# A four-layer graph network on one core: some transposes of the first and the last graphs by TensorE instead of through DRAM, and other turns at the end

## The chip, the cores and the metric

The kernel runs on one core of one Trainium2 chip. The metric is the device time of one execution in microseconds, as the median of several runs. Beside the runs there is one profiled execution, from which all busy times, waits and starts are taken.

A core has five engines that run at the same time, each with its own queue of instructions in a fixed order: PE (TensorE, matrix products, with a separate part for loading the stationary operand, PEld), DVE (VectorE), ACT (ScalarE, which needs a table load when it goes from one group of functions to another), POOL (GpSimd) and SP (SyncE, which here issues all DMAs). An instruction waits for semaphores that others raise; what stands behind it in its engine's queue waits too.

## The reference, cut to what matters

64 independent graphs of 256 nodes with 256 features pass through four layers. Everything is in 32-bit floating point. After each layer stands a residual sum and a layer norm.

```python
# layer 0: 4 heads, sigmoid attention, weighted by adj, normalized by the row sums
X, q, k = heads(lrelu(x @ W_lin + b)), heads(lrelu(x @ W_q)), heads(lrelu(x @ W_k))
adj_h = adj[:, None] * sigmoid(einsum('bhxd,bhyd->bhxy', q, k) * hd ** -0.5)
dis = deg ** -0.5                       # deg = adj_h.sum(-1), 0 where deg is 0
x = LN(x + LN(merge(dis[..., None] * adj_h * dis[..., None, :] @ X)) * g + b)
# layer 1: 8 heads, softmax attention masked by adj > 0
e = softmax(where(adj > 0, q @ k.T / sqrt(32), NEG))
x = LN(x + merge(e @ v) @ Wo + bo)
# layer 2: sum over neighbours, then a two-step network with RMS norm
agg = eps * x + adj @ x
x = LN(x + silu(rmsnorm(agg @ W1 + b1) * w) @ W2 + b2)   # W1 256 x 1024, W2 1024 x 256
# layer 3: additive attention, one head
Wh = x @ W;  e = leaky_relu(Wh @ a1 [:, None] + Wh @ a2 [None, :], 0.2)
x = LN(x + gelu(LN(softmax(where(adj > 0, e, NEG)) @ Wh) * gamma + beta))
```

## The kernel before, in words

**One graph.** `graph` writes down all operations of one graph `b`; a 256 x 256 matrix lies in one tile of 128 partitions with two halves of 256 elements side by side. Where a product needs its operand the other way round, the matrix has to be transposed. There are two ways in the code. `transposed` (L266) lets PE do it, as four products of 128 x 128 with the identity matrix (L263) into a PSUM tile, and `copy` (L297) has ACT bring that to SBUF (L299). `far_transposed` (L271) does it without PE: DVE transposes blocks of 32 x 32 (L275), and DMAs put the blocks in their places by way of a buffer in DRAM. For layer 3 these are four writes (L281) and four reads (L285); with `in_order=False`, for layer 0, one write (L289) and four reads (L291), and the two DVE products at L482 take up the order that is left.

Layer 0 gives the attention result of L475 to the second form (L478). Layer 1 makes the scores of four heads at a time (L510), DVE adds the mask and finds the least value (L395), ACT takes the exponential (L400), and each pair of heads goes through a DVE transpose (L521), one DRAM write of 512 KB (L523) and four reads of 128 KB (L525) before the product with v (L536). The reciprocals of the row sums are transposed by PE (L543) and spread over partitions through DRAM (L546, L549), L553 multiplies, and L319 applies Wo. Layer 2 is L567 (neighbours), L579 (W1), L609 and L613 (norm and SiLU), L622 (W2). Layer 3 sends its input through the first form (L628) and goes on with L637 (W and the two attention vectors), the exponentials (L400 again), a transpose of e by PE and ACT, the product with v, GELU (L661), the residual (L662), the last layer norm (L364) and the store (L664).

**The order of work.** `graph` only lists operations, with an estimated cost, the values that each reads and writes, and for those that need an ACT table a turn. `Plan.order` (L94) then makes one list for all 64 graphs before anything is emitted: it keeps a clock for each engine and always takes the operation that can start earliest by its estimates, the one with the earlier due time where they are equal. A due time is the least due time or turn of what comes after. `emit` (L714) writes the instructions in the order of the planned starts, and so each engine's queue is fixed.

A turn is `4 * min(b + ROUND[layer], plan.graphs - 1 + TAIL[layer]) + func`, with func 0 for sigmoid (layer 0), 1 for exponentials (layers 1 and 3), 2 for SiLU (layer 2), 3 for GELU (layer 3). ROUND = 0, 2, 5, 7 makes one round hold layer 0 of graph b, layer 1 of graph b - 2, layer 2 of b - 5 and layer 3 of b - 7, so that ACT changes its table once for each function and round. TAIL bounds the round at the end, so that the last graphs share turns: with 5 for layer 3, graph 60 has its exponentials in round 67 and graphs 61, 62 and 63 in round 68. An operation with a turn may not be planned before all ACT operations of earlier turns have been.

Operations that wait for nothing, which are the loads, are held back in another way:

```python
if (op.due - AHEAD if op.first else op.turn or 0) > turns[turn]:
    continue
```

AHEAD = 14 lets a load in when its due time is at most 14 turns away, where four turns are a round. Tiles come from pools with a fixed number of slots (SLOTS: 42 of the kind "s", 8 PSUM tiles "p", 8 DRAM buffers "h"), and an operation can't be planned before it has its slots.

Of the kernel before, what the change touches and what calls it, by code (L numbers as in the profile page):

```python
# [11 lines left out]
OP = mybir.AluOpType  # L12

P = 128
# [5 lines left out]
PE_MM, PE_TR = 432, 109  # L20
# [5 lines left out]
DMA_KB, DMA_SEEN = 4, 1900  # L26

WORDS = {"s": 516, "d": 1024, "b": 2048, "c": 32, "p": 512, "h": 1024}
AHEAD = 14

ROUND = 0, 2, 5, 7
TAIL = 0, 2, 3, 5
SLOTS = {"s": 42, "d": 10, "b": 3, "c": 72, "p": 8, "h": 8}


# [39 lines left out]
class Plan:  # L75
# [9 lines left out]
    def op(self, engine, cost, fn, w=(), r=(), turn=None, mode="full", after=None, size=0):  # L85
        pair = lambda x: x if isinstance(x, tuple) else (x, None)
        w, r = [pair(x) for x in w], [pair(x) for x in r]
        op = Op(engine, cost, fn, w, r, self.graph, turn, mode, after, size)
        op.table = turn is not None and engine == "ACT"
        if op.table:  # L90
            self.turns[turn] = self.turns.get(turn, 0) + 1
        self.ops.append(op)
# [73 lines left out]
def two(v):  # L166

    return v.t.rearrange("p (n c) -> p n c", n=2)
# [69 lines left out]
def graph(plan, nc, c, t, out, b):  # L238

    op = plan.op  # L240
    pe, dve, act, pool = nc and nc.tensor, nc and nc.vector, nc and nc.scalar, nc and nc.gpsimd
# [7 lines left out]
    def turn(layer, func):  # L249
        return 4 * min(b + ROUND[layer], plan.graphs - 1 + TAIL[layer]) + func  # L250

# [6 lines left out]
    def transpose(dst, src, w, r):  # L258

        def fn():  # L260
            for j in range(2):
                for i in range(2):
                    pe.transpose(dst()[:, j, i * P:(i + 1) * P], src()[:, i, j * P:(j + 1) * P], c.ident)  # L263
        op("PE", 4 * PE_TR, fn, [w], [r], mode="transpose")

    def transposed(src):  # L266
        ps = Value("p", "ps", 2)
        transpose(lambda: two(ps), lambda: two(src), ps, src)
        return ps

    def far_transposed(src, name, in_order=True):  # L271


        eb, far, dst = Value("s", "eb"), Value("h", "far", 4), Value("s", name, 4)
        op("DVE", 635, lambda: dve.transpose(  # L275
            eb.t.rearrange("p (b g i) -> p g b i", b=4, i=32),
            src.t.rearrange("p (n k w) -> p k n w", n=2, k=2)), [eb], [src])
        if in_order:
            F = lambda a: far.t[:64].rearrange("(a z) (y w) -> a (z y) w", a=4, w=P)[a]
            for a in range(4):  # L280
                op("SP", 420, lambda a=a: nc.sync.dma_start(  # L281
                    F(a).rearrange("(b j) w -> j b w", b=4),
                    eb.t[32 * a:32 * a + 32].rearrange("j (b w) -> j b w", b=4)), [(far, a)], [eb], after=3000, size=64)
            for a in range(4):
                op("SP", 420, lambda a=a: nc.sync.dma_start(  # L285
                    dst.t.rearrange("q (g a i) -> a q g i", g=4, a=4)[a],
                    F(a).rearrange("q (g i) -> q g i", g=4)), [(dst, a)], [(far, a)], after=4500, size=200)
            return dst
        op("SP", 420, lambda: nc.sync.dma_start(far.t[:, :512], eb.t), [(far, i) for i in range(4)], [eb], after=3000, size=256)  # L289
        for q in range(4):  # L290
            op("SP", 420, lambda q=q: nc.sync.dma_start(  # L291
                dst.t[32 * q:32 * q + 32].rearrange("j (a g) -> j a g", a=4),
                far.t[:, :512].rearrange("(a j) (b g) -> b j a g", a=4, b=4)[q]), [(dst, q)],
                [(far, i) for i in range(4)], after=4200, size=64)
        return dst

    def copy(ps, name):  # L297
        dst = Value("s", name, 2)
        op("ACT", 466, lambda: act.copy(dst.t, ps.t), [dst], [ps])  # L299
        return dst  # L300
# [109 lines left out]
    xT, adjT, x, adj = load("x0T", "xT"), load("adjT", "adjT"), load("x", "x"), load("adj", "adj")  # L410
    qk = []
    for w, name in ((c.w0_q, "qT0"), (c.w0_k, "kT0")):
        ps = feature_major(w, xT)
        y = Value("s", name)
# [3 lines left out]
    ps = token_major(xT, lambda: c.w0_l.t, [c.w0_l])  # L418
    v = Value("s", "v0")
# [20 lines left out]
    ps = Value("p", "ps")  # L440
# [18 lines left out]
    dp, dis = Value("c", "dp"), Value("c", "dis")  # L459
# [5 lines left out]
    by_head = lambda ap: ap.rearrange("p (g d) -> p g d", d=HD0)  # L465
    dis_b = lambda: dis.t[:, :8, None].to_broadcast([P, NB * H0, HD0])
    op("DVE", 603, lambda: dve.tensor_tensor(by_head(v.t), by_head(v.t), dis_b(), OP.mult), [v], [v, dis])
    ps = Value("p", "ps", 2)
# [6 lines left out]
                    pe.matmul(two(ps)[i * HD0:(i + 1) * HD0, hp, :], two(v)[:, m, h * HD0:(h + 1) * HD0],  # L475
                              A(h)[:, m, :], start=(m == 0), stop=(m == NB - 1))
    op("PE", 4 * PE_MM, fn, [ps], [v, att], mode="columns")
    yb = far_transposed(ps, "yT", in_order=False)  # L478
    y = Value("s", "y", 2)
    for i in range(2):  # L480
        by = lambda ap, i=i: ap.rearrange("p g (i k w) -> p g i k w", i=2, k=2)[:, :, i]
        op("DVE", 345, lambda y=y, i=i, by=by: dve.tensor_tensor(  # L482
            by(y.t.rearrange("p (g d) -> p g d", g=4)), yb.t.rearrange("p (i k g w) -> p i g k w", i=2, k=2, g=4)[:, i],
            dis.t[:, :8].rearrange("p (g i) -> p i g", i=2)[:, i, :, None, None].to_broadcast([P, 4, 2, 32]), OP.mult),
            [y], [yb, dis])
    mv, m = stats(y)
    affine(y, mv, m, c.g0, lambda n, xb=xb: two(xb)[:, n, :], [xb])
    x = normed(y, "x1")
# [5 lines left out]
    ps = feature_major(c.w1_q, xT)  # L494
# [5 lines left out]
    v1 = copy(token_major(xT, lambda: c.w1_v.t, [c.w1_v]), "v1")  # L500
    av, r = Value("p", "av", 2), Value("c", "r")
    eTs = []
    for hq in range(H1 // 4):
        pss = [Value("p", "ps", 2) for _ in range(4)]

        def fn(hq=hq, pss=pss):
            for n in range(NB):
                for i in range(4):
                    s = slice(i * HD1, (i + 1) * HD1)
                    pe.matmul(two(pss[i])[:, n, :], two(qT1)[s, hq, n * P:(n + 1) * P], two(kT1)[s, hq, :],  # L510
                              start=True, stop=True)
        op("PE", 2 * PE_MM, fn, pss, [qT1, kT1], turn=turn(1, EXP), mode="rows")
        for pair in range(2):


            e, eb, far, eT = Value("d", "e", 4), Value("d", "eb"), Value("h", "far"), Value("d", "eT", 4)
            for i in range(2):
                softmax(pss[2 * pair + i], negmask, HD1 ** -0.5, e,
                        lambda n, i=i, e=e: e.t[:, 256 * (2 * i + n):256 * (2 * i + n + 1)],
                        lambda n, i=i: 2 * i + n, r, lambda n, h=4 * hq + 2 * pair + i: 2 * h + n, turn(1, EXP))  # L520
            op("DVE", 1155, lambda e=e, eb=eb: dve.transpose(eb.t.rearrange("p (b g i) -> p g b i", b=4, i=32),  # L521
                                                             e.t.rearrange("p (g b i) -> p g b i", b=4, i=32)), [eb], [e])
            op("SP", 420, lambda eb=eb, far=far: nc.sync.dma_start(far.t, eb.t), [far], [eb], after=3500, size=512)  # L523
            for q in range(4):
                op("SP", 420, lambda far=far, eT=eT, q=q: nc.sync.dma_start(  # L525
                    eT.t[32 * q:32 * q + 32].rearrange("j (a g) -> j a g", a=4),
                    far.t.rearrange("(a j) (b g) -> b j a g", a=4, b=4)[q]), [(eT, q)], [far], after=4000, size=128)
            eTs.append(eT)


    def fn():
        for hq in range(H1 // 4):
            for m in range(NB):
                for i in range(4):
                    h = 4 * hq + i
                    pe.matmul(two(av)[i * HD1:(i + 1) * HD1, hq, :], two(v1)[:, m, h * HD1:(h + 1) * HD1],  # L536
                              eTs[h // 2].t.rearrange("p (a h n k i) -> p h k n a i", a=4, h=2, n=2, k=2)[:, i % 2, m],
                              start=(m == 0), stop=(m == NB - 1))
    op("PE", 4 * PE_MM, fn, [av], [v1, *eTs], mode="columns")

    op("DVE", 180, lambda: dve.reciprocal(r.t[:, :16], r.t[:, :16]), [r], [r])
    ps = Value("p", "ps")
    op("PE", PE_TR, lambda ps=ps: pe.transpose(ps.t[:16, :P], r.t[:, :16], c.ident), [ps], [r], mode="transpose")  # L543
    rT, far, rb = Value("s", "rT"), Value("h", "far"), Value("s", "rb", H1)
# [7 lines left out]
    yT = Value("s", "yT")  # L552
    op("DVE", 575, lambda: dve.tensor_tensor(yT.t, av.t, rb.t, OP.mult), [yT], [av, rb])  # L553
    x = normed(plus(token_major(yT, lambda: c.w1_o.t, [c.w1_o]), xb), "x2")

    adj2 = load("adj2", "adjT")
    for n in range(NB):
        d = lambda n=n: two(adj2)[:, n, n * P:(n + 1) * P]
# [4 lines left out]
    ps = Value("p", "ps", 2)  # L563
# [10 lines left out]
    for j in range(0, HB, 2):  # L574
        ps = Value("p", "ps", 2)
# [17 lines left out]
    ps = Value("p", "ps")  # L593
# [21 lines left out]
    ps = Value("p", "ps", 2)  # L615
# [9 lines left out]
    x = normed(plus(ps, xb), "x3")  # L625


    xT3 = far_transposed(x, "xT3")  # L628
    v3 = Value("s", "v3", 2)
    V3 = lambda: v3.full.rearrange("p (n c) -> p n c", n=2)  # L630
    s1 = lambda n: V3()[:, n, D:D + 1]
    for n in range(NB):
        ps = Value("p", "ps")
# [14 lines left out]
    e = Value("s", "e3", 2)  # L648
# [7 lines left out]
    eT = copy(transposed(e), "eT")  # L656
    ps = token_major(eT, lambda: V3()[:, :, :D], [v3])
    y3 = Value("s", "y", 2)
    mv, m = stats(ps, r3)
# [91 lines left out]
```

## Time and profile before

| | |
|---|---|
| median of 3 runs | 2822.43 us (2820.94 to 2826.75) |
| profiled execution | 2825.22 us |
| its span, first to last instruction | 2823.4 us |
| PE busy | 2752.3 us |
| DVE busy | 2494.3 us |
| ACT busy | 2131.5 us |
| mean DMA rate | 170 GB/s |
| DRAM reads and writes | 290.60 MB and 185.07 MB |
| mean granted PE clock | 0.991 |

In the lines of the timeline below, the first two numbers are start and duration in us, counted from the first instruction; then come the engine, the line of the code, the operation, what it writes and reads, its shape and how many of them follow each other. In brackets stand the engine's idle time just before, and what ended it. L numbers are lines of the kernel before. Busy times of PE are those of a pipeline and overlap a little; the granted clock is the share of its full speed that PE was given.

### The profile page before, as it was taken

The numbers are of one execution on the slowest core, as the hardware profiler recorded it, in microseconds if no ns is written. First come the engines' busy times: TensorE is split into PE (matmuls) and PEld (weight loads), VectorE is DVE, ScalarE is ACT, GpSimd is POOL, SyncE is SP. The second block draws the span as 40 slices with busy tenths as digits, with TensorE's granted clock in tenths as the row PEclk, the third lists the DMA queues.
The fourth block names the chain that finished last, engine by engine and source line by source line (L and its number), as shares of the span: only waits on it lengthen the run. The fifth ranks groups of instructions, "written<-read, shape, count | busy, mean of one in ns | idle before, by whom it ended". The sixth has DMA issues, their size and how long they took to land.

```text
span 2823.4 us, 55149 instructions
## 1 busy us (share of the span) xinstructions
PE 2752.3 (97%) x17092; PEld 2189.6 (78%) x17092; DVE 2494.3 (88%) x7757; ACT 2131.5 (75%) x5054; POOL 585.8 (21%) x902
## 2 busy tenths in 40 slices
PE   8899999999999999999999999999999999999996
PEld 6667777887787878788878878778787778777784
DVE  5788898989899998998899989899989989899975
ACT  3767787778688777877777777878768877686774
POOL 1011211212222222212212212222212221212111
PEclk9999999999999999999999999999999999999998
DMA  4857476646466646665576556556556647475641
GB/s 142 252 151 196 152 202 180 187 134 192 127 193 199 197 135 200 192 179 148 155 192 180 172 163 183 171 167 187 174 149 183 198 141 201 125 194 153 181 123 41
DMA packets 558613, 479.40 MB, mean 170 GB/s; under 512 B 184304, under 2 KB 516976, under 8 KB 558320
## 3 DMA queue, kind: packets, MB, share of 16 engines
q1 hardware_dynamic: 558320, 475.87, 59.2%
q8 instruction: 137, 2.24, 0.4%
q14 instruction: 156, 1.28, 0.2%
HBM read 290.60 MB, written 185.07 MB: 168 GB/s over the span
## 4 chain that ended last, share of the span: by engine, by line
PE 87%; DVE 5%; ACT 3%; DMA 2%; SPq 1%; issue 1%; POOL 0%; DVEq 0%; POOLq 0%; ACTq 0%
PE ps L622 15%; PE ps L308 15%; PE ps L319 14%; PE ps L579 14%; PE ps L510 4%; PE ps L432 4%; PE ps L567 4%; PE ps L637 4%; PE ps L475 3%; PE av L536 3%; PE ps L263 2%; ACT e L400 1%; PE ps L449 1%; DVE e L395 1%; DVE st L333 1%
## 5 line engine op out<-in xcount | busy, mean ns | idle before, releaser
L400 ACT ACTIVATE e<-e,low 128x256 f32<-128x256 f32 x1152 | 575.7, 501 | 73.5 <-DVE low L395 69.8
L622 PE MATMUL ps<-w,hT 128*128 128x256 f32 x2048 | 480.6, 382 | 4.2 <-ACT hT L613 4.2
L579 PE MATMUL ps<-aggT,w 128*128 128x256 f32 x2048 | 470.8, 382 | 2.8 <-ACT aggT L299 1.4
L345 POOL TENSOR_SCALAR mv<-mv 128x2 f32<-128x2 f32 x384 | 123.0, 320 | 1624.8 <-DVE mv L335 1074.0
L579 PEld LDWEIGHTS ps<-aggT,w 128*128 128x128 f32 x2048 | 382.4, 190 | 69.2 <-issue 8.6
L622 PEld LDWEIGHTS ps<-w,hT 128*128 128x128 f32 x2048 | 381.3, 190 | 67.6 <-issue 10.5
L395 DVE CUSTOM_DVE_ANT_0 e<-ps,adj 128x256 f32<-128x256 f32 x1024 | 361.7, 420 | 33.5 <-PE ps L510 32.5
L521 DVE STREAM_TRANSPOSE eb<-e 128x1024 f32<-128x1024 f32 x256 | 310.5, 1225 | 4.7 <-ACT e L400 4.0
L346 POOL TENSOR_TENSOR mv<-mv,mhalf 128x2 f32<-128x2 f32 x384 | 307.7, 801 | 32.0
L584 ACT ACTIVATE hT<-ps,b 128x256 f32<-128x256 f32 x512 | 225.8, 473 | 97.0 <-PE ps L579 66.6
L360 ACT ACTIVATE x<-y,mv 128x256 f32<-128x256 f32 x384 | 216.2, 599 | 61.3 <-DVE mv L356 53.2
L333 DVE BATCH_NORM_STATS2 st<-y 128x6 f32<-128x256 f32 x640 | 242.3, 412 | 1.4
L400 ACT ACTIVATION_READ_ACCUMULATOR e<-e,low 128x1 f32 x1152 | 220.8, 192 | 0.0
L609 DVE SCALAR_TENSOR_TENSOR hT<-hT,r,pr 128x256 f32<-128x256 f32 x512 | 207.3, 474 | 7.0 <-PE pr L606 6.6
L590 DVE TENSOR_TENSOR sq<-sq 128x512 f32<-128x512 f32 x192 | 130.5, 680 | 48.1 <-ACT sq L587 47.0
L438 DVE TENSOR_TENSOR att<-att,adjT 128x512 f32<-128x512 f32 x256 | 165.7, 678 | 5.6 <-ACT att L436 5.5
L587 ACT ACTIVATE sq<-hT 128x512 f32<-128x512 f32 x256 | 163.1, 637 | 2.0 <-DMA far<-eb 0.6
L510 PE MATMUL ps<-kT,qT 32*128 32x256 f32 x2048 | 152.0, 404 | 1.0 <-ACT kT L299 1.0
L462 POOL TENSOR_TENSOR dp<-dp,mhalf 128x8 f32<-128x8 f32 x64 | 109.2, 1707 | 202.7 <-DVE dp L461 175.4
L436 ACT ACTIVATE att<-ps 128x512 f32<-128x512 f32 x256 | 132.3, 603 | 25.0 <-PE ps L622 18.6
L613 ACT ACTIVATE hT<-hT 128x1024 f32<-128x1024 f32 x128 | 129.8, 1051 | 19.5 <-DVE hT L609 17.0
L308 PE MATMUL ps<-x0T,w_q 128*128 128x256 f32 x512 | 132.1, 392 | 7.2 <-DMA x0T<-in_xT 7.2
(108 smaller groups left out, 5526.7 us busy)
## 6 DMA issues: line engine op xcount, KB each, us to landing
far<-eb SPq DMA_DIRECT2D x256, 512.0 KB, 3.5
eT<-far SPq DMA_DIRECT2D x1024, 128.0 KB, 3.9
adj<-in_adj SPq DMA_DIRECT2D x128, 256.0 KB, 4.7
x0T<-in_xT SPq DMA_DIRECT2D x64, 256.0 KB, 3.5
adjT<-in_adjT SPq DMA_DIRECT2D x64, 256.0 KB, 4.4
x<-in_x SPq DMA_DIRECT2D x64, 256.0 KB, 4.8
adj<-in_adjT SPq DMA_DIRECT2D x64, 256.0 KB, 5.3
far<-eb SPq DMA_DIRECT2D x64, 256.0 KB, 2.7
```

What stands on the lines that cost most here:

```text
L308: pe.matmul(two(ps)[:, o, :], w.t[:, k, o * P:(o + 1) * P], two(xT)[:, k, :], start=(k == 0), stop=(k == DB - 1))
L319: pe.matmul(two(ps)[:, n, :], two(xT)[:, k, n * P:(n + 1) * P], w()[:, k, :], start=(k == 0), stop=(k == DB - 1))
L333: op("DVE", 328, lambda n=n: dve.bn_stats(st.t[:, 6 * n:6 * n + 6], two(src)[:, n, :]), [(st, n)], [(src, n)])
L346: pool.tensor_tensor(m()[:, :, 2], m()[:, :, 2], c.mhalf[:, :NB], OP.pow)
L360: op("ACT", 492, lambda n=n: act.activation(two(dst)[:, n, :], two(src)[:, n, :], AF.Identity, bias=m()[:, n, 0:1], scale=m()[:, n, 2:3]), ...
L395: op("DVE", 345, lambda n=n: dve.tensor_tensor_reduce(out=E(n), in0=two(logits)[:, n, :], in1=two(negmask)[:, n, :], scale=-scale, scalar= ...
L400: op("ACT", 491, lambda n=n: act.activation(E(n), E(n), AF.Exp, bias=low.t[:, n:n + 1], scale=-1.0, accum_out=r.t[:, col(n):col(n) + 1]), ...
L510: pe.matmul(two(pss[i])[:, n, :], two(qT1)[s, hq, n * P:(n + 1) * P], two(kT1)[s, hq, :], start=True, stop=True)
L521: op("DVE", 1155, lambda e=e, eb=eb: dve.transpose(eb.t.rearrange("p (b g i) -> p g b i", b=4, i=32), e.t.rearrange("p (g b i) -> p g b i" ...
L579: pe.matmul(two(ps)[:, i, :], c.w2_1.t[:, k, (j + i) * P:(j + i + 1) * P], two(aggT)[:, k, :], start=(k == 0), stop=(k == DB - 1))
L584: op("ACT", 357, lambda ps=ps, i=i, j=j: act.activation(Hb(j + i)[:, 0], two(ps)[:, i, :], AF.Identity, bias=c.b2_1.t[:, j + i:j + i + 1]) ...
L622: pe.matmul(two(ps)[:, n, :], Hb(j)[:, 0, n * P:(n + 1) * P], c.w2_2.t[:, j, :], start=(j == 0), stop=(j == HB - 1))
```

## The change

It sets new numbers and puts the other kind of transpose in three places. `NEAR = 1, 1, 3` says for how many graphs: layer 0 and layer 1 of the first graph (b = 0), layer 3 of the last three (61, 62, 63). All other graphs keep their way through DRAM.

In layer 0 of graph 0, ACT copies the result to SBUF, PE transposes it, and one DVE product with `dis` reads it from PSUM. In layer 1 of graph 0, each head of a pair is transposed by four PE transposes into PSUM and copied by ACT; eT then has another order of elements, so each entry of `eTs` now carries a function that picks its part. In layer 3 of the last three graphs, PE and ACT replace the whole of `far_transposed`. TAIL's last number goes from 5 to 4, so that graphs 60 to 63 all have layer 3 in round 67. AHEAD goes from 14 to 12 turns.

```diff
-AHEAD = 14
+AHEAD = 12
+NEAR = 1, 1, 3
 
 ROUND = 0, 2, 5, 7
-TAIL = 0, 2, 3, 5
+TAIL = 0, 2, 3, 4
...
     op("PE", 4 * PE_MM, fn, [ps], [v, att], mode="columns")
-    yb = far_transposed(ps, "yT", in_order=False)
     y = Value("s", "y", 2)
-    for i in range(2):
...
+    if b < NEAR[0]:
+        ps = transposed(copy(ps, "yT"))
+        op("DVE", 602, lambda ps=ps, y=y: dve.tensor_tensor(by_head(y.t), by_head(ps.t), dis_b(), OP.mult), [y], [ps, dis])
+    else:
+        yb = far_transposed(ps, "yT", in_order=False)
...
+            if b < NEAR[1]:
+                eT = Value("d", "eT", 2)
+                for i in range(2):
+                    half = lambda v, i=i: v.t[:, 512 * i:512 * (i + 1)].rearrange("p (n c) -> p n c", n=2)
+                    ps = Value("p", "ps", 2)
+                    transpose(lambda ps=ps: two(ps), lambda e=e, half=half: half(e), ps, e)
+                    op("ACT", 466, lambda ps=ps, eT=eT, half=half: act.copy(half(eT), two(ps)), [(eT, i)], [ps])
+                eTs.append((eT, lambda i, m, eT=eT: eT.t.rearrange("p (h m c) -> p h m c", h=2, m=2)[:, i, m]))
+                continue
...
-            eTs.append(eT)
+            eTs.append((eT, lambda i, m, eT=eT: eT.t.rearrange("p (a h n k i) -> p h k n a i", a=4, h=2, n=2, k=2)[:, i, m]))
...
-                              eTs[h // 2].t.rearrange("p (a h n k i) -> p h k n a i", a=4, h=2, n=2, k=2)[:, i % 2, m],
+                              eTs[h // 2][1](i % 2, m),
...
-    xT3 = far_transposed(x, "xT3")
+    xT3 = copy(transposed(x), "xT3") if b >= plan.graphs - NEAR[2] else far_transposed(x, "xT3")
```

More of the change, by code (lines that the diff above doesn't have):

```diff
@@ L477, in graph @@
     op("PE", 4 * PE_MM, fn, [ps], [v, att], mode="columns")
-    yb = far_transposed(ps, "yT", in_order=False)
     y = Value("s", "y", 2)
-    for i in range(2):
[L481 to L485, printed above, removed]
+    if b < NEAR[0]:
[4 more added lines that the diff above has]
+        for i in range(2):
+            by = lambda ap, i=i: ap.rearrange("p g (i k w) -> p g i k w", i=2, k=2)[:, :, i]
+            op("DVE", 345, lambda y=y, i=i, by=by: dve.tensor_tensor(
+                by(y.t.rearrange("p (g d) -> p g d", g=4)), yb.t.rearrange("p (i k g w) -> p i g k w", i=2, k=2, g=4)[:, i],
+                dis.t[:, :8].rearrange("p (g i) -> p i g", i=2)[:, i, :, None, None].to_broadcast([P, 4, 2, 32]), OP.mult),
+                [y], [yb, dis])
     mv, m = stats(y)
@@ L513, in graph @@
         for pair in range(2):
-            e, eb, far, eT = Value("d", "e", 4), Value("d", "eb"), Value("h", "far"), Value("d", "eT", 4)
+            e = Value("d", "e", 4)
             for i in range(2):
@@ L520, in graph @@
                         lambda n, i=i: 2 * i + n, r, lambda n, h=4 * hq + 2 * pair + i: 2 * h + n, turn(1, EXP))
+            if b < NEAR[1]:
+                eT = Value("d", "eT", 2)
+                for i in range(2):
+                    half = lambda v, i=i: v.t[:, 512 * i:512 * (i + 1)].rearrange("p (n c) -> p n c", n=2)
[4 more added lines that the diff above has]
+                continue
+            eb, far, eT = Value("d", "eb"), Value("h", "far"), Value("d", "eT", 4)
             op("DVE", 1155, lambda e=e, eb=eb: dve.transpose(eb.t.rearrange("p (b g i) -> p g b i", b=4, i=32),
@@ L536, in fn @@
                     pe.matmul(two(av)[i * HD1:(i + 1) * HD1, hq, :], two(v1)[:, m, h * HD1:(h + 1) * HD1],
-                              eTs[h // 2].t.rearrange("p (a h n k i) -> p h k n a i", a=4, h=2, n=2, k=2)[:, i % 2, m],
+                              eTs[h // 2][1](i % 2, m),
                               start=(m == 0), stop=(m == NB - 1))
-    op("PE", 4 * PE_MM, fn, [av], [v1, *eTs], mode="columns")
+    op("PE", 4 * PE_MM, fn, [av], [v1, *(eT for eT, _ in eTs)], mode="columns")
     op("DVE", 180, lambda: dve.reciprocal(r.t[:, :16], r.t[:, :16]), [r], [r])
```

## The prediction

> **What bounds the kernel now.** I read the page first: busy times and slices.
>
> ```profile
> span 2823.4 us, 55149 instructions
> ...
> PE 2752.3 (97%) x17092; PEld 2189.6 (78%) x17092; DVE 2494.3 (88%) x7757; ACT 2131.5 (75%) x5054; POOL 585.8 (21%) x902
> ...
> PEclk9999999999999999999999999999999999999998
> ```
>
> PE is busy 97% of the span, so a gain can only come from PE's idle time, 2823.4 - 2752.3 = 71.1 us, from time at a reduced clock, or from work taken off PE; this change adds PE work. Next I asked for the windows, to see where the 71 us lie. From 300 to 2500 us PE idles 6.0 us in all: the middle is full. From 0 to 300 us it idles 29.0, from 2550 on 35.7. So I read the windows of the start and then the timeline there. Columns: start:end and length, busy time of each engine with its instructions, clock, DMA share, GB/s.
>
> ```profile
> 50.00:75.00 25.00, 22.40 (x126) 17.59 (x122) 21.06 (x80) 12.69 (x32) 4.75 (x10) 0.93 0.07 22
> 75.00:100.00 25.00, 21.34 (x117) 15.81 (x117) 21.18 (x57) 21.12 (x63) 2.68 (x3) 0.80 0.95 271
> 100.00:125.00 25.00, 21.75 (x157) 14.12 (x153) 20.78 (x64) 18.37 (x49) 1.64 (x1) 0.93 0.85 247
> 125.00:150.00 25.00, 21.98 (x144) 15.55 (x144) 17.09 (x42) 9.26 (x19) 4.42 (x6) 1.00 0.94 275
> 150.00:175.00 25.00, 20.65 (x131) 16.18 (x134) 20.48 (x75) 12.86 (x33) 3.58 (x9) 0.93 0.26 67
> ```
>
> Here PE loses twice: it idles 2.60 + 3.66 + 3.25 + 3.02 + 4.35 = 16.9 us, and it runs at 0.80 to 0.93 after the gaps, which costs busy time times (1 - clock), 1.57 + 4.27 + 1.52 + 1.45 = 8.8 us. DMA is nearly full from 75 to 150. In the timeline, graph 0's own way shows why:
>
> ```profile
> 35.70 1.95 PE L475 MATMUL ps<-att,v 128*64 128x256 f32 x16
> 48.89 0.75 DVE L482 TENSOR_TENSOR y<-yT,dis 128x256 f32<-128x256 f32 x2
> 57.57 0.33 PE L263 MATMUL ps<-ident,x 128*128 128x128 f32 x1 [0.80 <-ACT x L360]
> 80.83 0.37 PE L543 MATMUL ps<-ident,r 128*16 128x128 f32 x1 [3.65 <-ACT att L436]
> 103.98 1.93 PE L536 MATMUL av<-eT,v 128*32 128x256 f32 x32
> 119.29 1.13 PE L319 MATMUL ps<-w_o,yT 128*128 128x256 f32 x4 [3.16 <-DVE yT L553]
> ```
>
> The layer-0 result leaves PE at 37.65 and is back from DRAM and in use at 48.89. The last exponential of graph 0 ends at 78.6, and its product starts at 103.98: 25 us in DRAM and in the queue of SP. The three bracketed idles (0.80, 3.65, 3.16) are PE waiting for graph 0 or having nothing else.
>
> The end, in the timeline again, for the graph that ends last (63):
>
> ```profile
> 2784.91 1.09 ACT L360 ACTIVATE x<-y,mv 128x256 f32<-128x256 f32 x2 [3.15 <-DVE mv L356]
> 2786.77 1.76 SPq L281 DMA_DIRECT2D far<-eb  x4
> 2788.64 2.54 SPq L285 DMA_DIRECT2D xT<-far  x4
> 2790.30 1.28 ACT L400 ACT_TABLE_LOAD   x1
> 2796.55 3.65 PE L637 MATMUL ps<-w,xT 128*128 128x258 f32 x8
> 2819.65 0.73 DVE L364 TENSOR_SCALAR o<-y,mv 128x256 f32<-128x256 f32 x2 [1.22 <-POOL mv L346]
> ```
>
> From x3 at 2786.00 to layer 3's first product at 2796.55 are 10.55 us; from there to the end of the span 26.9.
>
> **What the Trainium skill says.** "TensorE: Matmul & The Clock Gate", Part 1: an idle window of about 3.4 us halves PE's clock until it has been busy again. The trace agrees in kind: after the gap before 80.83 the window's clock is 0.80, and the 8 products at 59.57 took 3.52 us where the same 8 take 1.99 at 159.07. Part 4 there says a PE transpose goes to PSUM, so a copy follows, and doesn't count as PE activity in the same way; the trace has 273 ns as the median of one, and no run here tests the second point. "DMA: Bandwidth & Descriptors", Latency and other measured facts: HBM latency rises from 0.2 to 2 us at high load. The trace agrees in direction: the layer-1 writes take 3.5 us as a median and 4.95 at 83.70, where DMA is 95% full. "ScalarE: Activation LUTs", What ACT_TABLE_LOAD costs: 1.283 us and then a drain of 1.38. The trace has 1.28, but no drain: the load at 78.85 is followed by work at 80.15.
>
> **The change, part by part.**
>
> *Graph 0, layer 0.* Removed: one DVE transpose (0.72), five DMAs, two DVE products (0.75 together). Added: an ACT copy (0.58, row of L299), 4 PE transposes (0.60 for a group on its own, 0.45 in the chain) and one DVE product from PSUM (0.69, as L420). The way from 37.65 to 48.89 (11.2) becomes 0.58 + 0.60 and two handovers of 0.1, estimated from starts in the timeline: about 1.5. Graph 0 is 9 to 10 us earlier.
>
> *Graph 0, layer 1.* Removed: 4 DVE transposes of 1.23, so 4.9 us of DVE; 20 DMAs, at some 0.4 us of issue 8 us of SP, with 4 x (512 + 4 x 128) KB = 4 MB, which at the 271 GB/s of that window is 15 us of DMA. Added: 8 groups of 4 PE transposes and 8 ACT copies of 0.58 = 4.7 us. ACT has 12 us free in 50 to 75 and 4 in 75 to 100, so the copies fit, but they stand in ACT's queue among 16 exponentials at 0.5; where they fill that queue they cost up to 4.7. The 25 us from last exponential to product become about 2.
>
> *PE's price at the start.* 9 groups at 0.45 to 0.60: 4.0 to 5.4, taken as 4.7.
>
> *What the start gives back.* Holes that are graph 0's: 1.9 before 59.57 with 1.57 of clock, 3.65 before 80.83 with 4.27, 3.16 before 119.29 with 1.52: 16.1 us. Once graph 0 has passed them, its 8.6 us of layer-2 products (L567, L579, now at 128.84) can run there; but then they are gone later, and DVE is busy 20.5 to 21.2 of 25 us. I take that a third comes back as new holes: -11. Bounds: 0 (all come back) and -21 (of 25.7, when g3's exponentials, at 165 behind a DRAM queue that is now 4 MB shorter, come forward too). Net of PE: **-6.3**, from -16 to +4.7.
>
> *Layer 3 of graphs 61 to 63.* Removed: three DVE transposes of 0.70, 24 DMAs. Added: three groups on PE, three copies. For graph 63, 10.55 becomes a wait of about 0.35, 0.60, 0.58 and 0.06 = 1.6 (the same pair for e at 2804.57, 2805.21, 2805.85 takes 1.28): -9.0. The other two groups, 0.9 to 1.2, lie in the 3.22 us for which PE waits at 2771.63; without that cover, +1.2.
>
> *TAIL.* Graphs 60 to 63 share the last exponential and GELU turns, where 60 had its own before. Two table loads go (the one at 2790.30 stood in the chain; its 1.28 is inside the 10.55 already). But graph 60's GELU now waits for graph 63's exponentials, and its rest on DVE (plus 0.68, statistics 0.75 + 0.30, o 0.73 = 2.5) falls into the last stretch, where the chain is DVE's. Behind it in DVE's queue stands graph 63's own end. I take half, **+1.2** (0 to 2.5), as graphs 61 and 62 have moved forward. The end: **-7.8**, from -10.5 to -4.
>
> *AHEAD 14 to 12.* A load may start two turns later, half a round of 44 us (2823/64). The tightest is adjT, whose due time comes from layer 1's exponentials (turn 4b + 9): it is now let in at turn 4b - 3, three quarters of a round, 33 us, before the sigmoids of turn 4b that it multiplies. It landed in a median of 5.8 us from 1000 to 1150: 0. It also postpones W1 (1 MB) and loads into or past the crowded stretch, counted in the bounds above. For the middle: -3 (half of the 6.0 idle) to +6 (as much again).
>
> Sum: -6.3 - 7.8 + 0 = -14.1. The profiled execution took 2825.22 against its span of 2823.4, and the median is 2822.43, 2.8 lower; the difference carries over: 2822.4 - 14.1 = **2808.3**.
>
> **Rivals.**
>
> *Only the end gains.* The holes of the start come back in full, as DVE is at 85% there, and the transposes add part of their 4.7: +2 and -7.8, so about 2817. For it: the turns after graph 0 need graphs 1 to 3, which keep their DRAM ways. Against: PE's largest wait there is graph 0's.
>
> *The start gains more.* The crowded DMA from 75 to 150 is the cause of graph 3's late layer 1; 4 MB less brings all turns forward: -16 - 8, about 2798. For it: graph 3's write at 111.53 is read back only at 129.80. Against: DVE has the work anyway.
>
> *Slower.* With AHEAD at 12, PE has fewer loaded graphs from which to fill waits in the middle, and every round loses a little at layer 0's L308 or at L438 for adjT. It decides from (14.1 + 5.6) / 58 rounds = 0.34 us a round; at 0.35 it gives +20 - 14 = 2828. For it: the order of all work is planned anew. Against: from 300 to 2500 no DMA wait stands out in PE's list, and SP's loads of 1008 to 1013 are for work far later.
>
> **How the numbers follow.** Both ends gain: 0.55, own range 2800 to 2816. Only the end: 0.17. More at the start: 0.15. Slower or spoiled by a new order: 0.13. The range is 2796 to 2821: below lies half of the third case (0.07), above most of the last (0.12). What can be told from no change is 0.2%, 5.6 us: faster means under 2816.8. Faster: 0.54 + 0.08 + 0.15 + 0.01 = 0.78; same: 0.01 + 0.08 + 0.03 = 0.12; slower: 0.01 + 0.09 = 0.10.
>
> **What would show it.** Right: L482's place for graph 0 taken by a product from PSUM near 40; the first L536 near 75; clock at 0.9 or more in every 25 us window after 50; L637 of the last graph 2 us after its x; after 2770 two GELU loads instead of three. Wrong: new PE holes of 3 us from 120 to 200 (second case); PE idle from 300 to 2500 above 15 us, or DMA among PE's waits (slower case); DVE without a gap in the last 12 us and graph 63's o behind graph 60's work (end over-rated).

## The result and the profile after

The changed kernel takes 2791.23 us (median of 4 runs, 2789.09 to 2793.25) against 2822.08 for the one before: 30.9 us less, a ratio of 0.9887 with a 95% interval of 0.9870 to 0.9905. The prediction said 14 us less and 2796 as its lower end. The sign is right and the size is off by a factor of two. In the lines of this part, L numbers are those of the kernel shown. The profiled execution took 2789.26 us with a span of 2787.5; its page begins:

```profile
span 2787.5 us, 54969 instructions
...
PE 2739.8 (98%) x17140; PEld 2191.9 (79%) x17140; DVE 2483.4 (89%) x7748; ACT 2138.6 (77%) x5064; POOL 582.3 (21%) x902
```

PE has 48 instructions more and is busy 12.5 us less: it ran more of its work at full clock (the mean granted clock is 0.997, where it was 0.991). Its idle time fell from 71.1 to 47.7 us. The windows of the start, in the same columns as those of the kernel before:

```profile
50.00:75.00 25.00, 21.90 (x129) 16.52 (x128) 18.23 (x71) 18.38 (x49) 4.17 (x8) 0.93 0.53 143
75.00:100.00 25.00, 24.84 (x185) 18.43 (x184) 21.10 (x59) 20.03 (x53) 1.64 (x1) 1.00 0.40 122
100.00:125.00 25.00, 24.51 (x148) 18.61 (x148) 24.76 (x74) 21.47 (x58) 3.22 (x3) 1.00 0.88 262
125.00:150.00 25.00, 22.73 (x176) 17.48 (x172) 22.09 (x81) 11.32 (x26) 5.88 (x8) 1.00 0.85 238
150.00:175.00 25.00, 24.45 (x145) 19.75 (x144) 23.15 (x63) 20.76 (x51) 6.47 (x11) 1.00 0.85 240
```

From 50 to 175 us PE idles 3.10 + 0.16 + 0.49 + 2.27 + 0.55 = 6.6 us, where it was 16.9, and the clock is below 1 in one window only, which costs 21.90 x 0.07 = 1.5 us, where it was 8.8. The loss of the last of these windows, 4.35 us and its clock, which I had not put down to graph 0, is gone too. Graph 0's way, in the timeline:

```profile
33.47 1.95 PE L476 MATMUL ps<-att,v 128*64 128x256 f32 x16
...
36.49 0.60 PE L264 MATMUL ps<-ident,yT 128*128 128x128 f32 x4
...
37.17 0.68 DVE L482 TENSOR_TENSOR y<-ps,dis 128x512 f32<-128x512 f32 x1
...
47.56 0.60 PE L264 MATMUL ps<-ident,x 128*128 128x128 f32 x4
...
70.50 0.51 ACT L401 ACTIVATE e<-e,low 128x256 f32<-128x256 f32 x1
...
79.57 1.04 PE L264 MATMUL ps<-ident,e 128*128 128x128 f32 x8
80.44 0.27 PE L558 MATMUL ps<-ident,r 128*16 128x128 f32 x1
...
83.20 0.57 ACT L530 COPY eT<-ps 128x512 f32<-128x512 f32 x1
...
89.15 1.93 PE L551 MATMUL av<-eT,v 128*32 128x256 f32 x32
...
98.47 1.99 PE L320 MATMUL ps<-w_o,yT 128*128 128x256 f32 x8
```

The layer-0 result leaves PE at 35.42 and is in use at 37.17: 1.75 us, predicted 1.5, where it was 11.2. x1 is transposed at 47.56 instead of 57.57. Of these 10 us, 2.2 lie ahead of the change's work: the products of L476 themselves start 2.2 us sooner (in all the kernels below they start between 33.1 and 35.7).

The last exponential of graph 0 ends at 71.01 and its product starts at 89.15. That is 18.1 us, where it was 25 and the prediction had 2: the last of its transposes stand in PE's queue until 79.57, and the last copy in ACT's until 83.77. So the product comes 14.8 us sooner, where the prediction's two steps add up to 32. PE doesn't stand still in that time (it is busy 24.84 us of the window from 75 to 100), and at the steps shown none of the idles in brackets that stood there before is left. The end, for the graph that ends last:

```profile
2758.73 1.09 ACT L361 ACTIVATE x<-y,mv 128x256 f32<-128x256 f32 x2
...
2760.00 0.60 PE L264 MATMUL ps<-ident,x 128*128 128x128 f32 x4
...
2760.63 0.59 ACT L300 COPY xT<-ps 128x512 f32<-128x512 f32 x1 [0.55 <-PE ps L264]
...
2761.52 1.90 PE L652 MATMUL ps<-w,xT 128*128 128x258 f32 x8
...
2783.69 0.73 DVE L365 TENSOR_SCALAR o<-y,mv 128x256 f32<-128x256 f32 x2 [0.29 <-POOL mv L347]
```

From x3 (2759.82) to the product are 1.70 us, predicted 1.6; from there to the end of the span 26.0, where it was 26.9.

To compare kernels whose instructions stand in different orders, I use one more number, **lost time**: a point in time less what PE had done by then, its instructions counted at the rates of undisturbed stretches (a product of 128 x 256 at 0.216 us, as 16 of them in 3.45; a transpose at 0.11, as 4 in 0.44; and so on for each shape). It holds idle time, reduced clock and the small losses between unlike instructions. Transposes count as work in it, so the change's 36 at the start and 12 at the end have to be added, 4.0 and 1.3 us. It is read from the profiled execution alone, which in e3 lay 7.3 us from the median of its kernel, elsewhere less. It is good to some 2 us: for the kernels that do the same work as the one before, span less lost time comes to 2614.0 to 2617.5.

| lost, us | start, 0 to 300 | middle, 300 to 2500 | end |
|---|---|---|---|
| before | 58.7 | 94.0 | 55.2 |
| changed | 32.5 | 97.2 | 36.4 |
| difference with transposes | -22.2 | +3.2 | -17.5 |

The sum, -36.5, is that of the spans, -35.9. (The medians differ by less, as the profiled execution of the kernel before was 3.1 above its median and that of the changed one 2.0 below.) The prediction had -6.3, 0 and -7.8.

### The profile page after: what moved, and what is told of

Same layout as the page of the kernel before. It is cut to its first block, busy times and chain, and to the rows that moved or that the text cites. A ratio compares the mean times of both kernels' runs of the same rounds, so it can differ in the third digit from the quotient of the medians.

```text
span 2787.5 us, 54969 instructions
## 1 busy us (share of the span) xinstructions
PE 2739.8 (98%) x17140; PEld 2191.9 (79%) x17140; DVE 2483.4 (89%) x7748; ACT 2138.6 (77%) x5064; POOL 582.3 (21%) x902
## 4 chain that ended last, share of the span: by engine, by line
PE 87%; DVE 7%; ACT 3%; DMA 1%; issue 1%; POOL 1%; SPq 0%; DVEq 0%; POOLq 0%; ACTq 0%
PE ps L309 15%; PE ps L637 15%; PE ps L320 15%; PE ps L594 14%; PE ps L515 5%; PE ps L433 4%; PE ps L476 4%; PE ps L582 4%; PE av L551 4%; PE ps L652 3%; PE ps L264 2%; ACT e L401 1%; PE ps L450 1%; DVE eb L536 1%; DVE st L334 1%
```

## The experiments

The theories at the outset: **L**, graph 0 arrives sooner and so fills the start; **A**, what matters is that AHEAD keeps loads out of the crowded time; **T**, added later, the traffic that the other graphs are rid of; **D**, also later, the first exponential turn alone. Ratios are to the kernel before, run on the same chip beside each experiment, with 95% intervals. Where a number of AHEAD, NEAR or TAIL isn't named, it is that of the changed kernel.

**AHEAD alone, and all but AHEAD.**

```diff
-AHEAD = 14
+AHEAD = 12
```

> The kernel before with AHEAD at 12 and nothing else of the change. Theory L (graph 0 arriving sooner is what fills the start): no change, 2819 to 2825, PE idle of the first 300 us still near 29. Rival A (holding loads back by two turns keeps the crowded DMA of the start free): most of the start's gain, 2800 to 2808, PE idle of the first 300 us near 13 to 18.

Measured 2826.28, ratio 1.0004 (0.9997 to 1.0011): nothing. Lost time 59.3, 106.1, 43.2: no gain at the start, so A falls for the kernel before.

```diff
-AHEAD = 12
+AHEAD = 14
```

> The changed kernel with AHEAD back at 14. Theory L: as the changed kernel, 2788 to 2796. Rival A: most of the start's gain is lost, 2805 to 2815.

Measured 2804.38, ratio 0.9930 (0.9915 to 0.9945): in the range of neither theory, but most of the start's gain is there. AHEAD is worth nothing alone and 0.4% with the rest, each in one order. Lost time 38.4, 101.5, 38.0 against 32.5, 97.2, 36.4.

**Start alone, end alone**, both with AHEAD at 14 and the rest as before.

```diff
+NEAR = 1, 1, 0
```

> The kernel before with the PE transposes of graph 0 in layers 0 and 1 alone (AHEAD 14, the end as before). Theory L: the start's share alone, 2798 to 2804, PE idle of the first 300 us near 13 against 29. Rival A: little, 2814 to 2824. My prediction's own figure for the start was 6.3 less, 2816.

Measured 2814.29 (ratio 0.9956, 0.9942 to 0.9970). By its time it lies where the expectation had rival A. But the start lost 38.9 instead of 58.7, with AHEAD untouched, which speaks for the transposes; it is the middle that lost more, 100.6 instead of 94.0.

```diff
+NEAR = 0, 0, 3
-TAIL = 0, 2, 3, 5
+TAIL = 0, 2, 3, 4
```

> The kernel before with the end's part alone: layer 3 of the last three graphs by PE and the last turns shared (AHEAD 14, graph 0 as before). By the two traces the end gained 11 to 14 us: 2808 to 2812 by every theory of the start; by the prediction's figure of 7.8 it would be 2814. If the new order of the middle matters by itself, it lies outside 2804 to 2818.

Measured 2812.63 (0.9959, 0.9945 to 0.9973). Up to 2500 us it had lost the same as the kernel before (152.1 against 152.7); at the end 41.1 against 55.2. The queues of PE, DVE and ACT are the same in both up to 2655 us, so 14.1 - 1.3 = 12.8 us is what the end's part was worth on top of that course.

**One layer of graph 0 at a time.**

```diff
-NEAR = 1, 1, 3
+NEAR = 1, 0, 3
```

> The changed kernel with layer 1 of graph 0 back through DRAM, so that at the start only layer 0 of graph 0 is by PE. Theory L (graph 0 is simply early): layer 1 holds 23 of the 32 us by which graph 0 comes forward, so most of the start's gain goes, 2803 to 2812. Rival D (what counts is the first exponential turn, 10 us sooner, which layer 0 gives): nearly all of it stays, 2790 to 2797.

Measured 2814.12 (0.9953, 0.9938 to 0.9968). Slower than both ranges. The start lost 52.6. This speaks against D: the first table of exponentials is loaded at 57.5 us, 56.8 in the changed kernel, and most of the gain isn't there. But something else costs time here too. The largest wait of PE, in the waits of this kernel from 8 to 300 us (waiting engine and line, what it waited for, us in total, times, longest), is new:

```profile
PE ps L320 <- DMA w_v<-in_L_gnn_Wv: 7.3, 1, 7.3
```

A weight of layer 1 stands in SP's queue behind a write of exponentials, which waits for them until 66.93. With AHEAD at 12 the weight was let in that late; in the kernel before it was issued at 18.71. This is a cost of AHEAD that I had put at nothing, and with graph 0's layer 1 by PE there is no such write ahead of it (w_v is issued at 54.78 there).

```diff
-NEAR = 1, 1, 3
+NEAR = 0, 1, 3
```

> The changed kernel with layer 0 of graph 0 back through DRAM, so that at the start only layer 1 of graph 0 is by PE. Theory L: a third goes, 2795 to 2803. Rival D: most goes, 2805 to 2815.

Measured 2804.57 (0.9918, 0.9904 to 0.9933). The time lies between the two ranges. The start lost 45.2, though the first table of exponentials is loaded at 66.3 us, nearly as late as in the kernel before (67.2): so D falls. Before the price of the transposes, layer 0 alone gives 4 to 6 us at the start, layer 1 alone 11 to 14, both 23 to 26: together more than their sum, with the reservation that each is one order of the plan, and that layer 0 alone has the wait for the weight in it.

**Traffic without waiting.** The changed kernel, and for each pair of heads of graph 0 the old write and the four reads again, into tiles that nothing reads:

```diff
+                far, unread = Value("h", "far"), Value("d", "unread", 4)
+                op("SP", 420, lambda e=e, far=far: nc.sync.dma_start(far.t, e.t), [far], [e], after=3500, size=512)
+                for q in range(4):
+                    op("SP", 420, lambda far=far, unread=unread, q=q: nc.sync.dma_start(
+                        unread.t[32 * q:32 * q + 32].rearrange("j (a g) -> j a g", a=4),
+                        far.t.rearrange("(a j) (b g) -> b j a g", a=4, b=4)[q]), [(unread, q)], [far], after=4000, size=128)
                 continue
```

> The changed kernel, which in addition writes graph 0's exponentials to DRAM and reads them back in the old pattern (4 x 512 KB out, 16 x 128 KB in) into tiles that nothing reads; so the 4 MB and the 20 issues on SP are back, the waiting for them is not. Theory L: 2788 to 2796, as changed. Rival T (the gain is the traffic that graphs 1 to 3 are rid of): their DRAM ways are late again by up to 15 us, 2800 to 2810, with exponentials of graph 3 at 155 or later where the changed kernel has 142.

Measured 2819.94 (0.9976, 0.9965 to 0.9987), as slow as T said and slower. I took it for T. Then the same plan, each instruction in its place, with 256 bytes a row:

```diff
-                op("SP", 420, lambda e=e, far=far: nc.sync.dma_start(far.t, e.t), [far], [e], after=3500, size=512)
+                op("SP", 420, lambda e=e, far=far: nc.sync.dma_start(far.t[:, :64], e.t[:, :64]), [far], [e], after=3500, size=512)
...
-                        unread.t[32 * q:32 * q + 32].rearrange("j (a g) -> j a g", a=4),
-                        far.t.rearrange("(a j) (b g) -> b j a g", a=4, b=4)[q]), [(unread, q)], [far], after=4000, size=128)
+                        unread.t[32 * q:32 * q + 32, :64], far.t[32 * q:32 * q + 32, :64]), [(unread, q)], [far], after=4000, size=128)
```

> The kernel of e7_traffic with the same instructions in the same order on every engine and the same waits, but its additional transfers move 256 bytes of each row instead of 4096, 1024 or 4 x 1024: 0.3 MB instead of 4 MB. Rival T, as e7_traffic seems to show it (bytes on the DMA engines make the other graphs' transfers late): nearly all of e7's loss goes away, 2790 to 2802. If the 20 issues on SP, the slots that they take and the other order are the loss: 2812 to 2824.

Measured 2817.79 (0.9981, 0.9971 to 0.9990). T falls as a matter of bytes: a sixteenth of them costs the same. The start lost 49.4 with 4 MB and 50.0 without. Up to 100 us the dummies cost nothing: from 50 to 100 PE idles 3.1 us in the thin kernel, 3.3 in the changed one and 6.3 in the one before. From 100 to 175 it idles 13.6, 3.3 and 10.6, at clocks of 0.86, 1.00 and 0.95. The timeline of the thin kernel shows where:

```profile
122.17 0.72 DVE L276 STREAM_TRANSPOSE eb<-ps 128x512 f32<-128x512 f32 x1 [0.55 <-PE ps L476]
...
137.63 0.41 SPq L290 DMA_DIRECT2D far<-eb  x1
...
143.79 0.69 DVE L421 TENSOR_TENSOR v<-ps,b_l 128x512 f32<-128x512 f32 x1 [9.67 <-DMA far<-eb]
...
145.67 2.09 PE L515 MATMUL ps<-kT,qT 32*128 32x256 f32 x16 [6.99 <-ACT kT L300]
```

DVE has written eb at 122.9. SP comes to its DMA 14.7 us later, behind loads, reads and the dummies. DVE's next instruction, another graph's, waits for that DMA to land; it reads nothing of it, but both eb and its result take slots of the pool "s", so it most likely waits for the slot that eb gives free. DVE stands for 9.67 us, then PE for 6.99, and the clock of this window is 0.83. Of the 9.67, 3.5 pass before the DMA is issued and 6.1 until it has landed, in a window where the DMA engines are 86% busy with other transfers (the median landing of such a write is 2.7 us in the kernel before). What the dummies take away from the others is thus not the bandwidth of their own bytes. It is places in SP's queue, slots of tiles and the order, which the plan makes anew from about 70 us on; these three are not separated.

**The end's two parts.**

```diff
-TAIL = 0, 2, 3, 4
+TAIL = 0, 2, 3, 5
```

> The changed kernel with TAIL's last number back at 5, so that graph 60 has its own last turn. By the prediction's figures the shared turn costs 1.2 and saves nothing on the chain once the last graphs' layer 3 is early: 2788 to 2793. If sharing is what brought the end's gain: 2797 to 2804.

Measured 2800.08 (0.9907, 0.9890 to 0.9923): the end lost 45.3 instead of 36.4, as the expectation had it for the shared turn.

```diff
-NEAR = 1, 1, 3
+NEAR = 1, 1, 0
```

> The changed kernel with layer 3 of the last three graphs back through DRAM, the last turn still shared. By the prediction's figure the way from x3 to its product is 9 us longer for the graph that ends last: 2798 to 2804. If sharing the turn is what brought the end's gain (e8_own_turn lost 9), and the transposes little: 2790 to 2796.

Measured 2803.86 (0.9925, 0.9909 to 0.9941): the end lost 50.3, as the prediction's figure for the transposes had it. The queues are those of the changed kernel up to 2743 us, so the way can be read, in the kernel of this run:

```profile
2764.65 0.59 ACT L361 ACTIVATE x<-y,mv 128x256 f32<-128x256 f32 x1
...
2777.69 1.91 PE L652 MATMUL ps<-w,xT 128*128 128x258 f32 x8
```

From x3 at 2765.24 to the last graph's product are 12.45 us, where the changed kernel has 1.70; from there to the end of the span 25.8 and 26.0. So the transposes shorten the last path by the 9 us that were predicted, and a little more.

Each part seems worth 9 to 14 us, where both together were worth 12.8 on the course of e4. On the course of the changed kernel (e8 leaves it at 2630 us) the end with neither part was not run, so what both are worth there isn't known.

**AHEAD at 13, and a still shorter end.**

```diff
-AHEAD = 12
+AHEAD = 13
```

> The changed kernel with AHEAD at 13. AHEAD alone moved nothing, but at 14 the changed kernel lost 13. If 12 keeps loads out of a crowded time, 13 lies between: 2794 to 2802. If any other value only gives another order of all that follows, 13 may lie anywhere from 2788 to 2812, and the difference shows as PE idle in single places after 175 us and not as a DMA wait.

Measured 2812.15 (0.9952, 0.9934 to 0.9970): slower than both 12 and 14. Lost time 38.9, 107.3, 43.7. So 12 doesn't owe its time to loads kept out of a crowded time. PE's longest wait of the start is 4.3 us for v at L476, at 127 us and so sooner than expected, one place, and no DMA; with AHEAD at 14 (e2) the same place has 4.45. This fits AHEAD as a draw of another order. Against it stands that with both layers of graph 0 by PE, 13 and 14 lost 38 to 39 us at the start and 12 always less; these 4 to 6 us are not settled.

```diff
-NEAR = 1, 1, 3
+NEAR = 1, 1, 4
-TAIL = 0, 2, 3, 4
+TAIL = 0, 2, 2, 3
```

> A try for a faster end: TAIL 0, 2, 2, 3 and layer 3 of the last four graphs by PE, so that the last layers 2 and 3 share turns one round earlier. If what the shared turn saved is the way over another round of table functions: another 4 to 9 us less, 2782 to 2788. If the last stretch is DVE's work, which then is five graphs deep: same or slower, 2791 to 2800.

Measured 2789.83 (0.9878, 0.9863 to 0.9893), between the two ranges and not to be told from the changed kernel; the end lost 35.6. No version here beats it beyond doubt.

**The same work in another order.** One estimated cost of the planner is changed by a hair, in both kernels. Nothing that is computed changes; the queues of all engines do.

```diff
-PE_MM, PE_TR = 432, 109
+PE_MM, PE_TR = 433, 109
```

> The kernel before, with the planner's estimate of a product 433 ns for 432: the same operations in another order. If the order is luck of some 10 us: anywhere from 2812 to 2834, and its distance to the changed kernel with the same estimate is 10 to 20 us, near the predicted 14. If the 31 us are the change's own: 2820 to 2828, and 31 apart.

> The changed kernel with 433 for 432. Order is luck: 2795 to 2815, slower than the changed kernel, which had one of the good orders. The change's own: 2788 to 2794.

The same with 431:

> The kernel before with 431 for 432. As with 433: 2812 to 2834 if order is luck, 2820 to 2828 if not.

> The changed kernel with 431 for 432. As with 433: 2795 to 2815 if order is luck, 2788 to 2794 if not.

And, with the products at 432 again:

```diff
-DMA_KB, DMA_SEEN = 4, 1900
+DMA_KB, DMA_SEEN = 4, 1905
```

> The kernel before, with the planner's estimate of a transfer's landing 1905 ns for 1900. As the other orders of it: 2820 to 2828, with 54 to 60 us lost by 300 us.

> The changed kernel with 1905 for 1900. If the start's gain is the change's own and the middle is luck: 32 to 36 us lost by 300 us, and a time anywhere from 2790 to 2820, most likely near 2803.

| | before: median, lost at start, middle, end | changed: median, lost at start, middle, end | difference of medians |
|---|---|---|---|
| as given | 2822.08; 58.7, 94.0, 55.2 | 2791.23; 32.5, 97.2, 36.4 | -30.9 |
| 433 | 2825.37; 53.8, 106.6, 46.8 | 2808.39; 32.9, 104.4, 46.3 | -17.0 |
| 431 | 2822.51; 58.3, 102.3, 47.7 | 2819.93; 35.4, 116.9, 44.7 | -2.6 |
| 1905 | 2830.46; 56.1, 94.2, 58.7 | 2805.05; 34.0, 105.9, 45.1 | -25.4 |
| mean | 56.7, 99.3, 52.1 | 33.7, 106.1, 43.1 | -19.0 |

The ratios to the kernel before, as it was given, were 1.0005 and 0.9941, 0.9994 and 0.9983, 1.0020 and 0.9926. An estimate that is 1 ns off moves the changed kernel by up to 27 us (0.9983 against 0.9887), the kernel before by far less. Two times lie outside every range above: that of the changed kernel with 431 (2819.93) and that of the kernel before with 1905 (2830.46).

The rows are not all new orders at the start. With 1905 the changed kernel keeps the order that it was given up to 296 us, and the kernel before up to 1110; e8, e10 and e13 keep the changed kernel's up to 2580 us or more. Such repeats lost 32.5 to 35.8 at the start.

Where the 431 order loses, PE's waits from 300 to 2500 us show. First the changed kernel as given:

```profile
PE ps L612 <- DVE sq L607: 1.9, 5, 0.7
PE ps L594 <- DVE y L377: 1.6, 2, 0.8
```

and the same kernel with 431:

```profile
PE ps L637 <- ACT hT L599: 5.4, 2, 2.7
PE ps L637 <- ACT v L656: 4.1, 2, 2.1
PE ps L476 <- DVE v L468: 3.4, 4, 1.4
```

Eight waits in three kinds of place, up to 2.7 us long, on lines that the change doesn't touch in these graphs. PE's idle time in the middle is 9.8 us in the one and 22.6 in the other.

## Why the prediction was right or wrong

**The start was mis-sized, and this is the change's own.** The step that failed: "I take that a third comes back as new holes: -11", which after the price of the transposes left -6.3. In the kernels with both layers of graph 0 by PE and AHEAD at 12, three orders and four repeats, PE lost 32 to 36 us by 300. In those without the transposes of graph 0, four orders and two repeats, it lost 54 to 59. In the table the mean difference is -23.0, with 36 transposes -19.0; with AHEAD at 14 on both sides (e3) it is -19.8 and -15.8. Within these 300 us no third came back, and holes that I had given to other graphs closed as well: in the kernel as given the idle time of the start fell by 16.2 us and the loss by the clock, from 50 to 175 us, from 8.8 to 1.5. My outer bound was -16.

This was not because graph 0 came sooner than I had thought. Its exponentials reached their product 14.8 us sooner and not 32. I had looked for what waits for graph 0, and had not counted what waits behind graph 0's entries in the queue of SP. The kernel before has it in its trace. SP, with the DMAs that it issues there:

```profile
54.37 1.73 SPq L291 DMA_DIRECT2D yT<-far  x4
76.61 2.96 SPq L523 DMA_DIRECT2D far<-eb  x3
79.62 0.45 SPq L255 DMA_DIRECT2D x0T<-in_xT  x1
```

From 56.1 to 76.6 SP stands before the first write of graph 0's exponentials. The loads of other graphs are behind it, and so the DMA engines are 7% busy from 50 to 75 and 95% from 75 to 100. In the changed kernel these shares are 53% and 40%, and the first of them tells the two apart in every row of the table (7 to 9% against 53 to 55%). With AHEAD at 14 (e3) they are 23% and 48%. SP stands there too, but later, from 65 to 84.

How much of the 19 is graph 0's earlier arrival and how much the queue, stays open. Nothing shows PE's lost time to be due to these loads one by one. The thin dummies leave PE's gain from 50 to 100 us and take away all of that from 100 to 175. This fits an arrival that fills the first part and a queue that makes the second; but they do it in one order, and mainly in one stall.

**PE's price** was right in its size: with 48 transposes more, the groups of L264 hold 86.8 us against 80.6, 0.13 each, 4.7 for the 36 (4.0 by the rate of an undisturbed group). Whether the clock suffered from them is not shown, but from 61 to 69 PE did only transposes with gaps of up to 0.65 us, the window's clock is 0.93, and the 16 products that follow took 3.14 us, where such 16 take 2.00 elsewhere. The Trainium skill, "TensorE: Matmul & The Clock Gate", Part 4, says that transposes don't count as activity in the same way as products; this agrees with it, but the gaps, 3.1 us in all from 61 to 69, would explain it as well.

**The end was right on the mean.** -7.8 was predicted, the four pairs give 43.1 - 52.1 + 1.3 = -7.7. Such a close agreement is luck, as the pairs run from +0.8 to -17.5. The mechanism is shown by the path: the 1.6 us predicted from x3 to the product were 1.70, and 12.45 with the transposes left out (e10). The fourth graph's GELU, for which I had added 1.2, cost nothing that can be seen: the last stretch became 0.9 shorter. The pair as given shows -17.5, mostly because the changed kernel had a good order at its end (36.4 against 44.7 to 46.3 in the other rows of the table; e5 and e6, with the same end, lost some 32 and 33); the kernel before, with 55.2, lies within what its other orders have (43.2 with AHEAD alone, 46.8 to 58.7).

**The middle was not zero, and looks like a draw.** I bounded it by -3 and +6. It went from 94 to 107 in the kernel before and from 97 to 117 in the changed one. The rival "slower" named this, an order planned anew, but looked for its mechanism in late loads; no load stands among PE's larger waits there. At its largest, with 431, it took back 14.6 of the 20.6 us that start and end had given. On the mean the changed kernel loses 6.8 us more in the middle; with four orders each this can't be told from zero. So it can't be told either whether the third that I expected back came after 300 us.

So the change is worth some 19 us on the mean of four orders, and if that is its worth, the measured 31 hold about 12 of luck. The mean is loose: the four differences have a standard error of 6 us, and without the pair as given they come to 15. Against that mean, the prediction's 14 had 13 too little at the start and left out the 7 that the middle took back. Its range was too narrow, since it had no room for the order of middle and end, which moves the changed kernel by nearly as much as its whole gain.

**Of what was to be seen**, the first L551 came at 89 and not near 75: L558 and the exponentials of graph 1 stood between. This is the step "the 25 us become about 2", which were 18.1. The clock was 0.9 or more in the windows of the start, but not at the very end: it is one half from 2776 us on, as in the last 12 us of the kernel before. There are two GELU table loads at the end instead of three. The wrong-signs (holes of 3 us from 120 to 200, over 15 us of idle time in the middle) did not appear in the kernel as given. The sign for an over-rated end did in part: DVE has no gap above 0.3 us in its last 12 us of work, and yet the end was not over-rated.

## What to carry to other kernels

In a kernel whose order comes from a planner, each edit draws a new order of everything: change one estimate by 1 ns in both versions, a few times, before believing or tuning a difference of one per cent. Compare such kernels by stages, with PE's work counted and not by the clock, because a stage in which the difference of the two versions is alike over several orders shows what the edit itself does. When a transfer is taken out of an in-order queue, count who stood behind it, and who waited for the tiles that they held, and not only who waited for its data.

## What the runs showed that was not expected

Twenty DMAs of 256 bytes a row, in the place of twenty with 1 to 4 KB a row, left the loss as it was (50.0 against 49.4 us at the start). A tile whose DMA was issued 14.7 us after its data were ready and that took 6.1 us to land held up another graph's work, which reads none of it, for 9.67 us. One write that waits for its data kept SP from issuing anything for 20 us, with the DMA engines 7% busy, and 25 us at 95% followed. And the gaps of PE are dearer than their length: in the start of the kernel before, 16.9 us of gaps came with 8.8 us of reduced clock.
